# Loading and turning the first two context blocks during the folding stage of a Perceiver block

## The chip, the cores and the metric

The kernel runs on one core of a Trainium2 chip. Its engines work side by side, each through its own queue, in order: TensorE (PE in the profile; PEld is its weight load), VectorE (DVE), ScalarE (ACT), GpSimd (POOL) and SyncE (SP), which here only issues DMAs. ScalarE can issue DMAs too, from the same queue that holds its arithmetic. The metric is device time in microseconds (us), the median of several runs. The kernel before takes 2568.69 us (three runs, 2567.62 to 2571.4).

## The reference

`x` is 32 batches of 64 tokens with 256 channels; each batch has a context of 1601 keys with 192 channels. Three residual steps follow each other; only the first is touched by the change.

```python
x = x + xattn(layernorm(x), ctx, w_q, w_kv, w_out, b_out)
x = x + attn(layernorm(x), ...)      # a time-mixing recurrence over 64 tokens
x = x + ffn(layernorm(x), w1, b1, w2, b2)

def xattn(query, context, ...):      # 16 heads of 64
    q = query @ w_q                  # 256 -> 1024
    k, v = split(context @ w_kv)     # 192 -> 2 x 1024
    attn = softmax(q k^T / 8)        # per batch and head: 64 x 1601
    return (attn v) @ w_out + b_out
```

## The kernel before

Everything is float32. The keys are never projected. The key weights are folded into the queries instead: for each head, q (64 wide) times the transposed key weights gives a query of 192 channels, which meets the raw context. So the kernel has a first stage that folds, a long stage of attention, and a feed-forward stage at the end.

**Folding (`queries`, about 13 to 139 us).** The batches go in four groups of eight (`tg` = 0 to 3, 512 tokens each). A group has two halves (`e` = 0, 1) of eight heads. A half does, on TensorE: four head pairs projected (`q_ps`, L288), each copied out by ScalarE (L295) into one of five slots of the large tile `room[1]`; eight foldings onto the first 128 channels (`ql_ps`, L309), copied out in turn by VectorE (L316) and ScalarE (L317) into `q_lo`; the scores of the odd last key (`odd_ps`, L246) into `od`; and the foldings onto the other 64 channels (`qh_ps`, L337) into `q_hi`, mostly by VectorE (L344, L348). `q_ps` has two PSUM buffers, the others share six. `q_lo` (1 MB), `q_hi` (two halves of 0.5 MB) and `od` are stored to DRAM by SyncE (L319, L351, L260); `q_lo` and `q_hi` have two buffers each, so a copy waits for the store of the tile before the last. In the second half of groups 0, 1 and 2 the normalised x of the next group is turned (`xnT`, L208, L211), and VectorE normalises the group after that (L119 to L197).

**Context.** For every batch b the context comes three times: `ctx_load` (L143, tile `c`, 1152 KB, one buffer), used by the second product; `rows_load` (L152, four small DMAs) for the last 64 keys; and `blocks_load` (L170, tile `cb`, 12 DMAs of 96 or 104 KB in pieces of 128 bytes), which `ctx_prep` turns by four VectorE transposes (L368, L369) and one small DMA (L370) into `cT`, the context with channels on partitions, used by the scores. `q_load` (L180) brings the folded queries of a batch back.

**Attention (from about 139 us).** Two steps `u` per batch, eight heads each. A step computes scores in six pieces of 12 TensorE instructions (L654), each copied by ScalarE (L661) from one of two PSUM buffers; `rest_scores` (L631) takes one of these buffers too, in even steps between pieces 0 and 1. VectorE keeps a running maximum (L663 to L673), GpSimd reduces it over partitions (L680), VectorE subtracts it (L688, L699), ScalarE takes exponentials (L689, L700), VectorE sums (`total`, L773 to L777), GpSimd reduces the sum (L779), VectorE inverts it (`inverse`, L791 to L795), and a ScalarE-issued DMA stores the inverse (`keep`, L801). The products with the context follow one step later: `av_lo` (L464 with `c`, L816 with `rows`) and `av_hi` (L871, L826). Scores use two `s_sb` buffers; they are the same memory as `room[0]` and `room[1]`, and step 1 takes `room[1]`.

**What sets the order.** A scheduler orders each engine's instructions by program priority and data dependence; `tc.issue_after(x)` holds what stands under it until x has been issued in that order. All DMAs, from whichever engine, take eight completion counters in turn, and the compiled program makes a DMA wait until the DMA before it on its counter, eight back, has landed.

Of the kernel before, what the change touches and what calls it, by code (L numbers as in the profile page):

```python
# [15 lines left out]
P = 128  # L16
# [4 lines left out]
def kernel(  # L21
# [104 lines left out]
    with ExitStack() as st_b:  # L126
        with ExitStack() as st_a:
# [25 lines left out]
                            rows[b % 2][r0 : r0 + KR, n, n * C2 : P], ctx_768[b, KC * P : NK - 1, cs]  # L153
                        )

            def blocks_load(b):

                c = cpool.tile([P, NS, NBL, BL], F32, tag="cb", name=f"cb_{b}")
                for k in range(2):
                    n = (NB1, NBL)[k]
                    keys = slice(k * NB1 * BL, (k * NB1 + n) * BL)
                    for e in range(2):
                        a = 2 * k + e
                        for s in range(NS):
                            c0 = s * C2 + e * BL
                            nc.sync.dma_start(  # L170
                                c[a * BL : (a + 1) * BL, s, 0:n, :],
                                ctx_768[b, keys, c0 : c0 + BL].rearrange("(m q) r -> q m r", q=BL),
                            )
                return c
# [89 lines left out]
            def queries(tg, xnT, copied, sp, sps, wq_sb, wkT, room, codn, kodT, wk_lo, wk_hi, od):  # L264
# [7 lines left out]
                for e in range(NP // 4):  # L272
                    if e == 0 and more:
                        with tc.issue_after(copied.ins):
                            xn = normed_x(tg + 1, sp)
                    hi = sp.tile([P, QB, 4, T], F32, tag="q_hi", name=f"q_hi_{tg}_{e}", bufs=2)
                    qTs = []
                    for g in (2 * e, 2 * e + 1):
                        slot = (tg * NP // 2 + g) % 5
                        qT = room[1][:, slot * 2 * TG : (slot + 1) * 2 * TG].rearrange(  # L280
                            "p (k t) -> p k t", k=2
                        )
                        qTs.append(qT)
                        for k in range(2):
                            hp = 2 * g + k
                            pq = sps.tile([P, TG], F32, tag="ps", name=f"q_ps_{tg}_{hp}")
                            for c in range(2):
                                projected = nc.tensor.matmul(  # L288
                                    pq,
                                    lhsT=wq_sb[:, c, hp * P : (hp + 1) * P],  # L290
                                    rhs=xnT[:, c, :],
                                    start=(c == 0),
                                    stop=(c == 1),
                                )
                            nc.scalar.activation(qT[:, k, :], pq, AF.Copy, scale=HD**-0.5)  # L295
                    if e == 0 and tg == 0:
                        with tc.issue_after(projected.ins):
                            last_keys(codn, sps)
                    if e == 1 and more:
                        following = turned_x(tg + 1, xn, sp, sps)  # L300
                    for g, qT in zip((2 * e, 2 * e + 1), qTs):
                        lo = sp.tile([P, QB, 4, T], F32, tag="q_lo", name=f"q_lo_{tg}_{g}", bufs=2)
                        for k in range(2):
                            pl = [
                                sps.tile([P, QB, T], F32, tag="f", name=f"ql_ps_{tg}_{g}_{k}_{o}", bufs=6)
                                for o in range(2)
                            ]
                            for o in range(2):
                                nc.tensor.matmul(  # L309
                                    pl[o],  # L310
                                    lhsT=wkT[o * HD : (o + 1) * HD, 2 * g + k, 0:P],
                                    rhs=qT[o * HD : (o + 1) * HD, k, :],
                                    start=True,
                                    stop=True,
                                )
                            nc.vector.tensor_copy(lo[:, :, 2 * k, :], pl[0])  # L316
                            nc.scalar.copy(lo[:, :, 2 * k + 1, :], pl[1])  # L317
                        ns = slice(4 * g * T, (4 * g + 4) * T)
                        nc.sync.dma_start(  # L319
                            q_dram[tg][:, 0:P, ns].rearrange("b p n -> p b n"),  # L320
                            lo.rearrange("p b h t -> p b (h t)"),
                        )
                    all_q.append(qTs)
                    for n in (0, 1) if e == 1 and tg == 0 else (e,) if tg else ():
                        odd_scores(tg, n, kodT, all_q[n], od[n], sps)
                        if more:
                            odd_store(tg, n, od[n])
                        else:
                            odd_late.append(lambda n=n: odd_store(tg, n, od[n]))
                    for k in range(2):  # L330
                        ph = [
                            sps.tile([P, QB, T], F32, tag="f", name=f"qh_ps_{tg}_{e}_{k}_{o}", bufs=6)
                            for o in range(2)
                        ]
                        for n in range(2):
                            for o in range(2):
                                nc.tensor.matmul(  # L337
                                    ph[o][n * C2 : (n + 1) * C2, :, :],
                                    lhsT=wkT[o * HD : (o + 1) * HD, 4 * e + 2 * n + k, P:C],
                                    rhs=qTs[n][o * HD : (o + 1) * HD, k, :],  # L340
                                    start=True,
                                    stop=True,
                                )
                        nc.vector.tensor_copy(hi[:, :, 2 * k, :], ph[0])  # L344
                        if e == 1 and not more:
                            nc.scalar.copy(hi[:, :, 2 * k + 1, :], ph[1])
                        else:
                            nc.vector.tensor_copy(hi[:, :, 2 * k + 1, :], ph[1])  # L348
                    for n in range(2):
                        ns = slice((8 * e + 4 * n) * T, (8 * e + 4 * n + 4) * T)  # L350
                        store = nc.sync.dma_start(  # L351
                            q_dram[tg][:, P:C, ns].rearrange("b p n -> p b n"),
                            hi[n * C2 : (n + 1) * C2].rearrange("p b h t -> p b (h t)"),
                        )
                    if e == 0 and tg == 0:
                        for n in range(2):
                            projected_keys(n, wk_lo, wk_hi, kodT, sps)
                return following, store

            def ctx_prep(b):  # L360
# [12 lines left out]
            with tc.tile_pool(name="setup", bufs=1) as sp, tc.tile_pool(  # L373
# [11 lines left out]
                ]  # L385
                wk_hi, codn = wk_hi[0:C2], codn[0:B]
                kodT = kodT.rearrange("p (h b) -> p h b", b=B)
                od = kp.tile([P, NS * KT], F32, tag="cT", name="od")
                od = [
                    od[:, k * 2 * TG : (k + 1) * 2 * TG].rearrange("p (o t) -> p o t", o=2)  # L390
                    for k in range(2)
                ]
                wq_sb = wq_sb.rearrange("p (c n) -> p c n", c=2)
                wkT = wkT.rearrange("p (h c) -> p h c", c=C)
                wqr = w_q.rearrange("(c p) n -> p c n", p=P)
# [10 lines left out]
                for n in range(4, NT, 4):  # L406
                    nc.sync.dma_start(x_sb[:, n : n + 4, :], xr[:, n : n + 4, :])
                b_tiles = {0: blocks_load(0)}
                odd_late = []
                for g in range(NP // 2):  # L410
                    ps = sps.tile([P, 2, C], F32, tag="ps", name=f"wkT_ps_{g}")
                    for k in range(2):
# [8 lines left out]
                for tg in range(B // QB):  # L421
                    turned, store = queries(tg, *turned, sp, sps, wq_sb, wkT, room, codn, kodT, wk_lo, wk_hi, od)
                    if tg == 1:
                        q_tiles = {0: q_load(0)}
                        cT = ctx_prep(0)

            nats = {}
            aw = st_a.enter_context(tc.tile_pool(name="late", bufs=1))
# [539 lines left out]
                        x_sb[:, i, :], x_sb[:, i, :], bias_rows[:, 0, :], ALU.add  # L968
                    )

            c_tiles = {}
            rests = [None, None]
            last = None
            before = None
# [2 lines left out]
            for u in range(2 * B):  # L977
# [2 lines left out]
                phase, i = (u - 5) % 4, (u - 5) // 4  # L980
                if before is not None:
                    before.out()
                if j == 0:
                    rows_load(b)
                out, mixer, older = outs[max(i, 0)], mixers[max(i, 0)], mixers[max(i - 1, 0)]
                fill = {}
# [29 lines left out]
                s_sb, mx, top, done = scores(u, cT, q_tiles[b], hooks)  # L1016
                if j == 0 and b + 1 < B:
                    with tc.issue_after(store.ins):
                        b_tiles[b + 1] = blocks_load(b + 1)
                        q_tiles[b + 1] = q_load(b + 1)  # L1020
                mb = max_all(u, mx)
                if u == 1:
                    with tc.issue_after(top.ins):
                        cT_next = ctx_prep(1)
                if last is not None:
                    last.av_lo(fill, done)
                parts = exps(u, s_sb, rests[j], mb)
# [6 lines left out]
                    last.inverse()  # L1034
                    last.keep()
                if j == 0 and 0 < b < B - 1:
                    cT_next = ctx_prep(b + 1)
                elif j == 1:
                    cT = cT_next
                if phase == 0 and i > 0:  # L1040
# [4 lines left out]
                    out.vproj()  # L1045
                if phase == 1 and i >= 0:
                    mixer.norm()
                if j == 0:
                    c_tiles[b] = ctx_load(b)
                if phase == 3 and i >= -1:  # L1050
                    odd_load(i + 1)
# [150 lines left out]
```

## Time and profile before

| | |
|---|---|
| median of three runs | 2568.69 us |
| the profiled execution's own time | 2567.18 us |
| its span in the trace | 2565.4 us |
| TensorE busy | 2541.8 us, 99% |
| VectorE busy | 1925.2 us, 75% |
| ScalarE busy | 985.6 us, 38% |
| DMA on average | 68 GB/s; 190 GB/s over the first 230 us |

The page cuts the span in 40 slices; only the first three or four touch folding and the start of attention. Busy time is an average over stages. For a change at one place one asks what TensorE waits for at that place and which chain of work ends last there, in a window of the trace. "SPq" and "ACTq" are the queues of SyncE and ScalarE issuing DMAs. An arrow `<-` in a list of waits names what ended the wait.

### The profile page before, as it was taken

To read this page: it belongs to the slowest core of one execution; us is meant where nothing else is said; L and a number is where in the kernel's file an instruction comes from. 1 tells how busy PE (TensorE), PEld (TensorE's weight loads), DVE (VectorE), ACT (ScalarE), POOL (GpSimd) and SP (SyncE) were. 2 spreads that over 40 slices of the span, in tenths; PEclk is the share of its full clock that TensorE was granted. 3 is DMA by queue.
4 is the path that set the end of the run, shared out by engine and by line. 5 is a ranking of instruction groups with operands and counts; after the bars stand their busy time and mean duration, and the time that the engine had idled before them with its cause. 6 is when DMAs were issued, how large, how long until landed. Compare 5 with 4: busy or idle time off the path is not lost.

```text
span 2565.4 us, 38180 instructions
## 1 busy us (share of the span) xinstructions
PE 2541.8 (99%) x15650; PEld 1223.3 (48%) x15650; DVE 1925.2 (75%) x2364; ACT 985.6 (38%) x1104; POOL 410.7 (16%) x372
## 2 busy tenths in 40 slices
PE   9999999999999999999999999999999999999999
PEld 4334444444444444444444454444454444444466
DVE  5377777878787878878787878878787878787731
ACT  3343434334333434434433344343443334344221
POOL 1002111111111111111111111111111111111100
PEclk9999999999999999999999999999999999999999
DMA  7897332333232233233332323333332322310100
GB/s 189 225 210 112 62 62 51 66 65 65 53 69 56 49 58 65 47 66 66 65 63 57 61 40 65 54 59 66 65 65 53 69 55 48 62 45 4 53 13 21
DMA packets 435968, 174.24 MB, mean 68 GB/s; under 512 B 334960, under 2 KB 421520, under 8 KB 435792
## 3 DMA queue, kind: packets, MB, share of 16 engines
q1 hardware_dynamic: 435408, 171.53, 32.9%
q8 instruction: 123, 2.02, 0.3%
q14 instruction: 53, 0.43, 0.1%
q10 hardware_dynamic: 384, 0.26, 0.0%
HBM read 141.07 MB, written 29.10 MB: 66 GB/s over the span
## 4 chain that ended last, share of the span: by engine, by line
PE 90%; DVE 4%; issue 2%; SPq 1%; DMA 1%; POOL 1%; ACT 1%; ACTq 0%; DVEq 0%; POOLq 0%
PE s_ps L654 35%; PE o_lo L464 24%; PE o_hi L871 11%; PE y_ps L464 2%; PE q_ps L288 2%; PE h_ps L1113 2%; PE fy L1127 2%; PE rest_ps L631 2%; PE o_hi L826 1%; PE v_ps L924 1%; PE ql_ps L309 1%; DVE s_sb L699 1%; PE o_lo L816 1%; PE v_ps L938 1%; POOL den L779 1%
## 5 line engine op out<-in xcount | busy, mean ns | idle before, releaser
L654 PE MATMUL s_ps<-q,cT 64*128 64x512 f32 x4608 | 1008.1, 591 | 2.4 <-ACT s_sb L661 1.5
L654 PEld LDWEIGHTS s_ps<-q,cT 64*128 64x128 f32 x4608 | 443.7, 187 | 516.2 <-issue 497.5
L464 PE MATMUL o_lo<-s_sb,c 128*64 128x512 f32 x3024 | 680.3, 597 | 5.4 <-DMA c<-in_ctx_dram 5.4
L661 ACT COPY s_sb<-s_ps 128x1024 f32<-128x1024 f32 x384 | 388.3, 1011 | 744.8 <-PE s_ps L654 736.7
L699 DVE TENSOR_TENSOR s_sb<-s_sb,mb 128x2048 f32<-128x2048 f32 x192 | 431.5, 2284 | 0.0
L700 ACT ACTIVATE s_sb<-s_sb 128x2048 f32<-128x2048 f32 x192 | 367.2, 1913 | 123.6 <-DVE s_sb L699 123.6
L464 PEld LDWEIGHTS o_lo<-s_sb,c 128*64 128x64 f32 x3024 | 209.5, 137 | 387.0 <-issue 382.7
L665 DVE TENSOR_TENSOR m<-m,s_sb 128x1024 f32<-128x1024 f32 x256 | 312.3, 1220 | 45.4 <-ACT s_sb L661 24.2
L871 PE MATMUL o_hi<-s_sb,c 128*64 128x256 f32 x3024 | 337.7, 380 | 0.0
L776 DVE TENSOR_TENSOR t<-t,s_sb 128x1024 f32<-128x1024 f32 x256 | 311.9, 1218 | 8.6 <-DVE t L776 0.5
L871 PEld LDWEIGHTS o_hi<-s_sb,c 128*64 128x64 f32 x3024 | 217.9, 137 | 136.7 <-issue 37.1
L779 POOL PARTITION_ALL_REDUCE den<-t x64 | 207.1, 3236 | 400.2 <-issue 374.6
L791 DVE STREAM_TRANSPOSE turned<-den 128x512 f32<-128x512 f32 x64 | 45.5, 711 | 271.0 <-POOL den L779 271.0
L689 ACT ACTIVATE rest<-rest 128x512 f32<-128x512 f32 x64 | 40.4, 631 | 402.2 <-DVE rest L688 360.0
L680 POOL PARTITION_ALL_REDUCE mb<-m x64 | 114.2, 1785 | 427.4 <-DVE m L673 427.4
L688 DVE TENSOR_TENSOR rest<-rest,mb 128x512 f32<-128x512 f32 x64 | 44.3, 692 | 108.0 <-POOL mb L680 107.9
L619 POOL MEMSET rest<- 64x256 f32 x128 | 39.2, 307 | 418.3 <-PE o_lo L816 322.1
L368 DVE STREAM_TRANSPOSE cT<-cb 128x768 f32<-128x768 f32 x96 | 89.5, 957 | 0.0
L663 DVE TENSOR_TENSOR m<-s_sb 128x1024 f32<-128x1024 f32 x64 | 75.8, 1184 | 13.7 <-ACT s_sb L661 13.7
L816 PE MATMUL o_lo<-rest,rows 64*128 64x256 f32 x252 | 81.2, 402 | 0.0
L826 PE MATMUL o_hi<-rest,rows 64*128 64x256 f32 x252 | 81.2, 402 | 0.0
L111 POOL TENSOR_TENSOR rstd_ln<-rstd_ln,root 128x1 f32<-128x1 f32 (+1 forms) x24 | 33.1, 1380 | 296.9 <-DVE rstd_ln L110 279.1
(164 smaller groups left out, 1843.0 us busy)
## 6 DMA issues: line engine op xcount, KB each, us to landing
q<-q_dram SPq DMA_DIRECT2D x64, 768.0 KB
c<-in_ctx_dram SPq DMA_DIRECT2D x32, 1152.0 KB
cb<-in_ctx_dram SPq DMA_DIRECT2D x192, 104.0 KB
cb<-in_ctx_dram SPq DMA_DIRECT2D x192, 96.0 KB
q_dram<-q_lo SPq DMA_DIRECT2D x16, 1024.0 KB
q_dram<-q_hi SPq DMA_DIRECT2D x16, 512.0 KB
rows<-in_ctx_dram SPq DMA_DIRECT2D x64, 32.0 KB
rest<-o_dram SPq DMA_DIRECT2D x128, 1.0 KB
```

The costliest lines, as they stand in the source:

```text
L464: last = nc.tensor.matmul(out[rs], lhsT=lhsT[:, rs], rhs=rhs, start=start, stop=stop, skip_group_check=True,)
L654: done = nc.tensor.matmul(ps[:, k, :], lhsT=cT[rs, s, i * P : (i + 1) * P], rhs=q[rs, s, js : js + HALF], start=(s == 0), stop=(s == NS - 1),)
L661: copied = nc.scalar.copy(s_sb[:, 2 * i : 2 * i + 2, :], ps)
L665: nc.vector.tensor_tensor(m2, m2, s_sb[:, 2 * i : 2 * i + 2, :], ALU.max)
L680: nc.gpsimd.partition_all_reduce(mb, mx, P, bass_isa.ReduceOp.max)
L699: nc.vector.tensor_tensor(s, s, m, ALU.subtract)
L700: nc.scalar.activation(s, s, AF.Exp)
L776: nc.vector.tensor_tensor(t2, t2, p[:, 2 * i : 2 * i + 2, :], ALU.add)
L779: nc.gpsimd.partition_all_reduce(self.den, t2[:, 0, :], P, bass_isa.ReduceOp.add)
L816: nc.tensor.matmul(self.po[:, k * HH : (k + 1) * HH], lhsT=self.rows[lo, 0, :], rhs=self.rest[lo, k * HH : (k + 1) * HH], start=(k == 0), ...
L826: nc.tensor.matmul(self.ph, lhsT=self.rows.rearrange("p n c -> p (n c)")[hi, c0 : c0 + P], rhs=self.rest[hi, (1 - k) * HH : (2 - k) * HH], ...
L871: nc.tensor.matmul(self.ph[o * C2 : (o + 1) * C2, :], lhsT=self.ctx[:, self.at[c], P:C], rhs=self.s_sb[:, c, o * HH : (o + 1) * HH], start ...
```

## The change

`blocks_load` can take its room and its issuing queue from the caller. The blocks of batch 1 are loaded during group 0 of the folding, by 12 DMAs issued from ScalarE right after its copies into `q_lo` of the first half; they lie in a buffer of the tag `q`. `rows_load(0)` and `ctx_load(0)` are written at the end of group 2, where nothing that they need is late, and SyncE's compiled order has them, with the rows of batch 1, between the stores of group 0's two halves. `ctx_prep` runs for batch 0 after group 1 and for batch 1 after group 2, behind the last `q_hi` copies; in the kernel before, VectorE turned batch 0 within group 0 and batch 1 in step 1 of the attention, right after the maximum (`top`). The odd scores no longer lie in a `cT` buffer: the even half uses the memory of the running maximum `m2` (for group 3 a slot of `room[1]`), the other half the end of `room[1]`; in group 3 the even half is stored at once. The projections of a half (L288) may not be issued before the first folding of the half before (`folds`); in the kernel before the scheduler had moved them up between foldings, up to 11 matmuls at a time, where a half has eight. In the attention the loads that have gone are left out, and `ctx_prep(2)` waits for the maximum of step 2.

```diff
-            def blocks_load(b):
-                c = cpool.tile([P, NS, NBL, BL], F32, tag="cb", name=f"cb_{b}")
+            def blocks_load(b, room=None, queue=nc.sync):
+                if room is None:
+                    c = cpool.tile([P, NS, NBL, BL], F32, tag="cb", name=f"cb_{b}")
+                else:
+                    c = room.rearrange("p s n -> p (s n)")[:, 0 : NS * NBL * BL].rearrange(
+                        "p (s m r) -> p s m r", s=NS, r=BL
+                    )
...
-                            nc.sync.dma_start(
+                            queue.dma_start(
                                 c[a * BL : (a + 1) * BL, s, 0:n, :],
...
-                            for c in range(2):
-                                projected = nc.tensor.matmul(
+                            with tc.issue_after(folds[-1].ins) if folds else ExitStack():
+                                for c in range(2):
+                                    projected = nc.tensor.matmul(
...
-                                nc.tensor.matmul(
+                                fold = nc.tensor.matmul(
                                     pl[o],
...
-                            nc.scalar.copy(lo[:, :, 2 * k + 1, :], pl[1])
+                            laid = nc.scalar.copy(lo[:, :, 2 * k + 1, :], pl[1])
+                        if g == 2 * e:
+                            folds.append(fold)
...
                     for n in (0, 1) if e == 1 and tg == 0 else (e,) if tg else ():
+                        if not more and n == 0:
+                            at = (tg * NP // 2 - 1) % 5 * 2 * TG
+                            od[0] = room[1][:, at : at + 2 * TG].rearrange("p (o t) -> p o t", o=2)
                         odd_scores(tg, n, kodT, all_q[n], od[n], sps)
-                        if more:
+                        if more or n == 0:
                             odd_store(tg, n, od[n])
...
-                        nc.vector.tensor_copy(hi[:, :, 2 * k, :], ph[0])
+                        filed.append(nc.vector.tensor_copy(hi[:, :, 2 * k, :], ph[0]))
...
                             projected_keys(n, wk_lo, wk_hi, kodT, sps)
+                        cb = kp.tile([P, NS, H * T], F32, tag="q", name="cb_1")
+                        with tc.issue_after(laid.ins):
+                            b_tiles[1] = blocks_load(1, cb, nc.scalar)
...
-                od = kp.tile([P, NS * KT], F32, tag="cT", name="od")
-                od = [
-                    od[:, k * 2 * TG : (k + 1) * 2 * TG].rearrange("p (o t) -> p o t", o=2)
-                    for k in range(2)
-                ]
+                m2 = ap.tile([P, 2, HALF], F32, tag="m2", name="od")
+                od = [m2, room[1][:, 10 * TG : 12 * TG].rearrange("p (o t) -> p o t", o=2)]
...
                     if tg == 1:
                         q_tiles = {0: q_load(0)}
-                        cT = ctx_prep(0)
+                    if tg in (1, 2):
+                        with tc.issue_after(filed[-1].ins):
+                            cTs[tg - 1] = ctx_prep(tg - 1)
+                    if tg == 2:
+                        rows_load(0)
+                        c_tiles = {0: ctx_load(0)}
...
-            c_tiles = {}
+            cT, cT_next = cTs[0], cTs[1]
...
-                if j == 0:
+                if j == 0 and b:
                     rows_load(b)
...
                     with tc.issue_after(store.ins):
-                        b_tiles[b + 1] = blocks_load(b + 1)
+                        if b:
+                            b_tiles[b + 1] = blocks_load(b + 1)
                         q_tiles[b + 1] = q_load(b + 1)
                 mb = max_all(u, mx)
-                if u == 1:
-                    with tc.issue_after(top.ins):
-                        cT_next = ctx_prep(1)
...
                 if j == 0 and 0 < b < B - 1:
-                    cT_next = ctx_prep(b + 1)
+                    with tc.issue_after(top.ins) if b == 1 else ExitStack():
+                        cT_next = ctx_prep(b + 1)
...
-                if j == 0:
+                if j == 0 and b:
                     c_tiles[b] = ctx_load(b)
```

## The prediction

> **What bounds the kernel now.** I read the page first. TensorE is busy nearly all the time, so time can only come from its gaps and its slow stretches.
>
> ```profile
> span 2565.4 us, 38180 instructions
> PE 2541.8 (99%) x15650; PEld 1223.3 (48%) x15650; DVE 1925.2 (75%) x2364; ACT 985.6 (38%) x1104; POOL 410.7 (16%) x372
> ```
>
> Then the list of what TensorE waited for up to 204 us, where the change lies (us, times, longest), and the table by stretch (the last three numbers: granted clock, DMA share, GB/s).
>
> ```profile
> PE o_lo L464 <- DMA c<-in_ctx_dram: 5.4, 1, 5.4
> ...
> PE ql_ps L309 <- ACT q_lo L317: 1.2, 1, 1.2
> PE rest_ps L631 <- DMA cT<-cT: 1.1, 1, 1.1
> PE ql_ps L309 <- DVE q_lo L316: 1.0, 1, 1.0
> ...
> PE s_ps L654 <- ACT s_sb L661: 0.6, 1, 0.6
> 160.00:180.00 20.00, 14.56 (x68) 6.27 (x66) 17.71 (x15) 11.46 (x10) 2.01 (x2) 0.89 0.95 179
> ```
>
> The late `c` costs 5.4 us, and after that gap the clock is halved for a while: the 48 instructions of `o_lo` at 178.36 take 12.54 us, against 10.45 at 324 us. It looks as if 5.4 + 2.1 + 1.1 + 0.6 = 9.2 us were to be had. The chain that ends last says otherwise (start, us, what):
>
> ```profile
> 181.04 2.69 DVE cT L368 x3
> 183.76 0.37 DVE cT L369
> 184.17 0.69 DVE rest L688
> 184.86 6.60 DVE s_sb L699 x3
> ...
> 193.90 0.70 DVE t L777
> 194.76 3.23 POOL den L779
> ...
> 201.26 0.20 ACTq L801
> 201.50 1.02 ACT s_sb L661
> 202.57 13.14 PE s_ps L654 x60
> ```
>
> From 162 to 194.6 VectorE works without a pause; then come the sum over partitions, the inverse, and its store, which is a ScalarE instruction and stands before the first score copy of step 2. TensorE can't go past piece 0 and `rest_ps` without that copy. So VectorE's work, not `c`, decides when TensorE runs freely again, at 202.57.
>
> Last, the place where the new DMAs go: ScalarE's and TensorE's order around 30 us, and what SyncE waited for at 160 to 204 us.
>
> ```profile
> 25.28 0.58 ACT L317 COPY q_lo<-ql_ps 128x512 f32<-128x512 f32 x1 [0.27 <-PE ql_ps L309]
> 33.07 0.60 ACT L295 ACTIVATE room<-q_ps 128x512 f32<-128x512 f32 x1 [7.20 <-PE q_ps L288]
> ...
> 31.05 7.13 PE L288 MATMUL q_ps<-xnT,room 128*128 128x512 f32 x16
> ...
> SPq L444 <- DMA wv_lo<-in_L_xattn_w_kv_dram: 3.4, 1, 3.4
> SPq L260 <- DMA c<-in_ctx_dram: 3.2, 1, 3.2
> ```
>
> ScalarE is free for 7.2 us between two copies. The last two lines show DMAs held by others with which they share no data: each waits for the landing of the DMA eight before it.
>
> **The change, part by part** (+ is longer).
>
> *Start of step 2: -2.3.* The four transposes leave VectorE at 181.04 (3.1 us). Next late is the maximum over partitions: GpSimd has it at 181.31 + 1.78 = 183.1. In the new order a sum (L776, 1.24) fills part of that gap: sum to 182.3, L688 183.1 to 183.8, L699 to 190.4, sum to 191.7, L777 to 192.3, against 194.6. All behind it moves with it: TensorE at 200.3. Ends: -0.8 if the sum did not move up, -3.1 if the maximum came early.
>
> *The clock there: +2.1.* With `c` there, TensorE does the products from 172.9 at full rate (the exponentials that they read end at 170.7, 173.4 and 176.1, each ahead of its third): 10.45, then 5.2, to 188.5, then 0.6 + 2.6 + 1.5 of last rows, piece 0 and `rest_ps`, to 193.2. Then it idles 7.1 us, longer than the gap that cost 2.1, so I take 2.1; ends 0 and 3.4 (6.8 us of halved clock before, all of it used). The Trainium skill (TensorE: Matmul & The Clock Gate, Part 1) says that an idle window of about 3.4 us, running freely, halves the clock; the two halved windows after the 5.4 us gap agree. It speaks against the full gain, since the gap is moved, not removed: by it the sum below stands, and without it the sum would be 2.1 less.
>
> *Folding order: -2.3 and +1.7.* The two waits of 1.2 and 1.0 stand behind projections that were moved up, and go. But in the second halves of groups 0 and 1 VectorE now puts three `q_lo` copies (0.62 each) among the normalising, 1.9 us in 1.2 us of idle, so it ends at 46.05 for 45.34, and the fourth copy at 46.7. The buffer of that copy is wanted by `qh_ps`, which without projections in between is due at 45.8: 0.9 and 0.8. Ends 0 (copies hide) and 2.4.
>
> *The 12 DMAs on ScalarE: +4.7, and +1.0 of clock.* They stand between the copy that ends at 25.86 and the one due at 33.07. By the compiled order ScalarE's first waits for nothing late, but SyncE's eleventh block DMA of batch 0 now stands eight behind it, the first `q_lo` store comes after that on SyncE, and ScalarE's twelfth stands eight behind this store. So: first issued at 25.9, landed about 28.6 (the first weights, a larger load, took from 0.72 to 3.62); two block DMAs and the store issue until 30; the store landed 5.15 after issue (24.30 to 29.45 by the landing marks), so at 35.0 if nothing shares the DMA engines. What shares: block DMAs landed 0.76 apart, a 1 MB store took 3.9, so eleven plus two blocks and the store in a row end at 27.8 + 9.9 + 3.9 = 41.6. Middle 38.3. ScalarE then issues (0.3) and copies (0.6); TensorE, whose two `q_ps` buffers are full at 34.5, goes on at 39.2: 4.7, ends 1.4 and 8.0. A gap of this length costs half of the 2.1; ends 0 and 2.1. Behind ScalarE's DMAs wait the four `q_ps` copies and, through them, every folding of the half. The Trainium skill (DMA: Bandwidth & Descriptors, Issuing engines are not separate DMA queues) says that a second issuing engine saves issue time alone, since all DMAs share 16 engines. By that sentence alone the term would be 8.0 and the sum +8.9; no row of this run has two engines issuing much at once, so it can't be weighed closer here.
>
> *More in the DMA queues: +0.7.* `cb` (1.2 MB), `c` (1.15 MB) and eight row DMAs move into 26 to 50 us; SyncE issues nothing between 31 and 46.7, which covers the issues. What they push back are stores whose tiles are reused; VectorE waited 2.7 for such stores. I take a quarter; ends 0 and 2.7.
>
> *At nothing:* the eight transposes in groups 1 and 2 stand in the 6.9 us of four projections, where VectorE idled 5.0 or more after its copies; without that cover they would cost 3.1 each. ScalarE's first copy of step 1 (159.66) must now wait for four late odd stores in `room[1]`; they should land near 152, behind the last stores and `q_1`, and if they came after 159.7 each us would count. GpSimd's queue is as before, and the clearing that the row loads wait for (L107) is done at the start. The reloads for batches 2 and 3 come earlier, under steps in which TensorE never waited.
>
> Sum: -2.3 + 2.1 - 2.3 + 1.7 + 4.7 + 1.0 + 0.7 = +5.6. The profiled execution is 2567.2, 1.5 below the median; 2568.7 + 5.6 = 2574.3.
>
> **The rivals.**
>
> *The hold is short (not slower).* If the store lands at 35.0, TensorE goes on at 35.9: hold 1.4, no halved clock, no late stores: -2.3 + 2.1 - 2.3 + 1.7 + 1.4 = +0.6, 2569.3. For it: SyncE's issues cost 0.5 and the DMA engines are idle at 25 us. Against: nine more block DMAs are issued in that time. It decides where the store lands before 36.
>
> *The hold is long and stores fall behind.* 8.0 + 2.1 + 2.7 in place of 4.7 + 1.0 + 0.7: +12.0, 2580.7. For it: a DMA share of 0.8 to 0.98 in most of 60 to 160 us. Against: 0.50 at 40 to 60.
>
> *The whole 9.2 is won.* If VectorE's chain did not hold TensorE at step 2, then with a short hold: -9.2 - 2.3 + 1.7 + 1.4 = -8.4, 2560.3. Against: the chain above, link by link.
>
> **How the numbers follow.** A measurement can tell about 0.2%, 5.1 us, so slower begins at 2573.8 and faster at 2563.6. My forecast, own range 2570 to 2578, 0.50: its middle lies just above the bound, slower 0.29, within 0.21. Short hold 0.22: within 0.20, faster 0.02. Long hold 0.19: slower. Whole gain 0.09: faster 0.08, within 0.01. Together slower 0.48, within 0.42, faster 0.10. A range of 2566 to 2581 leaves out the whole gain, the far end of the short hold, and a little above.
>
> **What would show it.** ScalarE's first `q_ps` copy of group 0's second half starts at 36 to 41 (before 33.07), and TensorE's list has a wait of 1.4 to 8 for it there. No wait for `c` or for the turned context. TensorE waits some 7 us for `s_sb` L661 at the start of step 2, with a halved clock behind it. A free run through step 2, or ScalarE back by 34, would make the prediction wrong.

## Result and profile after

The changed kernel takes 2576.77 us in the median of seven runs (2573.37 to 2579.62), the kernel before 2568.69 on the same chip (seven runs, 2565.27 to 2573.22). The ratio is 1.0027, with a 95% interval of 1.0018 to 1.0037: slower by a little, and inside the predicted range. The profiled execution took 2574.45 us; its span of 2572.6 us is 7.2 us longer than that of before. TensorE is as full as it was: 2543.4 us busy, 99%.

What TensorE waited for in the changed kernel up to 300 us (total, times, longest):

```profile
PE s_ps L672 <- ACT s_sb L679: 7.9, 1, 7.9
PE q_ps L294 <- ACT room L301: 5.1, 1, 5.1
...
PE qh_ps L349 <- DVE q_lo L322: 1.9, 2, 1.1
```

The waits for `c`, for `cT` and for `q_lo` under `ql_ps` are gone. In their place stand 7.9 us at the start of step 2, 5.1 us behind the new DMAs, and 1.9 us before `qh_ps`. Both long ones begin at ScalarE. Its timeline in the changed kernel (start, duration, queue or engine, line, operation; in brackets the idle time before and what ended it):

```profile
25.38 15.57 ACTq L175 DMA_DIRECT2D cb<-in_ctx_dram  x12
41.00 1.09 ACT L301 ACTIVATE room<-q_ps 128x512 f32<-128x512 f32 x2 [15.04 <-DMA cb<-in_ctx_dram]
```

And TensorE's timeline there:

```profile
31.14 5.40 PE L294 MATMUL q_ps<-xnT,room 128*128 128x512 f32 x8
41.65 5.73 PE L294 MATMUL q_ps<-xnT,room 128*128 128x512 f32 x8 [5.12 <-ACT room L301]
```

Issuing the twelve DMAs keeps ScalarE for 15.6 us. The chain of the changed kernel in this window (start, us, what) says why:

```profile
26.98 1.94 ACTq L175
...
28.96 6.34 DMA cb<-in_ctx_dram
...
35.32 5.65 DMA cb<-in_ctx_dram
...
41.00 0.61 ACT room L301
```

ScalarE's last DMAs wait for the landing of other block DMAs, twice in a row, 6.3 and 5.7 us. The other place is the start of step 2, seen in ScalarE's timeline:

```profile
205.75 0.22 ACTq L819 DMA_DIRECT2D pd_dram<-rden  x1
206.01 1.01 ACT L679 COPY s_sb<-s_ps 128x1024 f32<-128x1024 f32 x1 [6.84 <-DVE rden L813]
```

and in TensorE's:

```profile
207.07 16.09 PE L672 MATMUL s_ps<-q,cT 64*128 64x512 f32 x60 [7.89 <-ACT s_sb L679]
```

TensorE has its data and stands 7.9 us at a copy that is queued behind the store `keep`; its clock is then halved, and the sixty score instructions take 16.09 us where they took 13.14 before. In the table by stretch (the last three numbers: granted clock, DMA share, GB/s) the clock is 0.74 there:

```profile
200.00:220.00 20.00, 12.93 (x48) 5.60 (x50) 13.66 (x18) 5.41 (x8) 6.31 (x4) 0.74 0.18 40
```

Where the 7.2 us come from, by the two traces (the line from first projection to first `xnT` is the second half of group 0):

| stretch | before | after | difference |
|---|---|---|---|
| start to that first projection | 31.05 | 31.14 | +0.1 |
| that projection to the first `xnT` of group 1 | 6.97 | 16.08 | +9.1 |
| from there to the first scores (rest of the folding) | 101.64 | 98.41 | -3.2 |
| first scores to step 2's sixty | 62.91 | 61.44 | -1.5 |
| step 2's sixty | 13.14 | 16.09 | +2.95 |
| sum | | | +7.4 |

### The profile page after: what moved, and what is told of

Its sections match the earlier page's. It is cut to its first block, busy times and chain, and to the rows that moved or that the text cites. A ratio compares the mean times of both kernels' runs of the same rounds, so it can differ in the third digit from the quotient of the medians.

```text
span 2572.6 us, 38172 instructions
## 1 busy us (share of the span) xinstructions
PE 2543.4 (99%) x15650; PEld 1223.5 (48%) x15650; DVE 1925.9 (75%) x2364; ACT 986.1 (38%) x1104; POOL 411.5 (16%) x372
## 4 chain that ended last, share of the span: by engine, by line
PE 90%; DVE 4%; issue 2%; DMA 2%; POOL 1%; SPq 1%; ACT 1%; ACTq 0%; DVEq 0%; POOLq 0%
PE s_ps L672 35%; PE o_lo L482 24%; PE o_hi L889 11%; PE y_ps L482 2%; PE q_ps L294 2%; PE h_ps L1130 2%; PE fy L1144 2%; PE rest_ps L649 2%; PE o_hi L844 1%; PE v_ps L942 1%; DVE s_sb L717 1%; PE ql_ps L315 1%; PE o_lo L834 1%; PE v_ps L956 1%; POOL den L797 1%
```

## Experiments

My theory: the twelve DMAs cost their hold of ScalarE and nothing else, and step 2 starts when ScalarE gets past `keep`, whatever has been loaded. The rivals: the extra transfers themselves cost; the new order on TensorE costs; the wait for `c` was on the path. Differences to the changed kernel are between medians; each comparison with the kernel before is against runs of it on the same chip. The kernel before had medians of 2568.69 to 2572.48 us in these sets of runs, so a difference between medians from two sets is sure to a few us only.

### The order alone, and the hold on top of it

The order alone, in the kernel before:

```diff
-                            for c in range(2):
-                                projected = nc.tensor.matmul(
+                            with tc.issue_after(folds[-1].ins) if folds else ExitStack():
+                                for c in range(2):
+                                    projected = nc.tensor.matmul(
...
-                                nc.tensor.matmul(
+                                fold = nc.tensor.matmul(
...
+                        folds.append(fold)
```

> The kernel before with the order on TensorE alone changed to the changed kernel's: projections never between the two foldings of a pair; no load is moved. My theory: the folding stretch from the first group's xnT to the first scores shrinks from 101.6 by about 3 us (1 to 4), and all of it reaches the end: 3 us under the kernel before. Rival, that the shorter stretch in the changed kernel came from the hold ahead of it (queues filled while TensorE stood): no change within 1 us.

Measured: 2570.24 us (11 runs), ratio 1.0004 (0.9993 to 1.0015). No change, but not for the rival's reason. TensorE's order is now that of the changed kernel; VectorE's is not. The scheduler keeps it as it was, with the copies into `q_lo` behind the whole normalising of the next group. TensorE's timeline in this run:

```profile
46.76 1.64 PE L310 MATMUL ql_ps<-room,room 64*128 64x512 f32 x2 [2.92 <-DVE q_lo L317]
48.34 3.05 PE L246 MATMUL odd_ps<-room,room 64*32 64x512 f32 x32
```

The stretch from the first `xnT` to the scores is 102.34 us. In it are 3.9 us of waits for `q_lo` and about 1.6 of slow clock (1.64 for 1.12, 3.05 for 1.95). What the regular order gains, VectorE's order takes.

The hold on top, in that kernel (its other loads held at their places with `issue_after(store.ins)`):

```diff
+                        cb = kp.tile([P, NS, H * T], F32, tag="q", name="cb_1")
+                        with tc.issue_after(laid.ins):
+                            blocks_load(1, cb, nc.scalar)
```

> The kernel before with the regular order of foldings (every projection follows the last folding) and the twelve block DMAs issued from ScalarE at the changed kernel's place, into a query buffer that nothing reads; the kernel's own loads all stay where they were. My theory: ScalarE held for about 15 us, TensorE idle about 5 us with its clock halved on both sides, about 9 us over the same kernel without the twelve DMAs (the run with the order alone), so about 6 us over the kernel before. Rival, that the hold is covered and the changed kernel loses elsewhere: within 2 us of the run with the order alone.

Measured: 2577.85 us (8 runs), ratio 1.0028 (1.0017 to 1.0038); 7.6 us over the order alone. ScalarE's queue is held 16.89 us, TensorE stands 4.88, and the first `xnT` comes at 48.69 where it came at 38.70. Of these 10.0 us, 1.2 lie ahead of the projections (32.89 for 31.73) and are not the hold's; 3.8 come back in the folding (98.51 for 102.34): with the DMAs in ScalarE's queue, the scheduler puts VectorE's copies among the normalising, as in the changed kernel, and TensorE no longer waits for them. The hold is the loss, and a better order of VectorE comes with it.

### The blocks on SyncE's queue

```diff
-                            b_tiles[1] = blocks_load(1, cb, nc.scalar)
+                            b_tiles[1] = blocks_load(1, cb, nc.sync)
...
-                        if g == 2 * e:
-                            folds.append(fold)
+                        folds.append(fold)
```

> The changed kernel with one thing different: the twelve DMAs of the second batch's blocks are issued from SyncE's queue instead of ScalarE's (the order on TensorE is pinned to that of the changed kernel by making every projection follow the last folding). My theory, ScalarE held by its own issues: the gap of 5.1 us before the second eight projections and the halved clock around it go, the stretch from the first projections to the next xnT falls from 16.1 to about 7 us, the time is about 9 us under the changed kernel's (about 1 under the kernel before's). Rival 1, the extra transfers themselves cost: the stretch stays above 14 us and the time stays within 2 us of the changed kernel's. Rival 2, SyncE's queue is now too full and its query stores come late: the stretch falls, but waits of up to 9 us for the copies into q_lo appear in the folding.

Measured: 2579.32 us (5 runs), ratio 1.0034 (1.0021 to 1.0047): no gain at all. The hold is gone (first `xnT` at 39.18, no wait before the projections), as the theory said, though the sixteen projections take 8.83 us and not the 7 expected; but the folding behind it takes 107.7 us for 98.4. The waits:

```profile
PE ql_ps L315 <- DVE q_lo L322: 5.8, 2, 2.9
PE s_ps L671 <- ACT s_sb L678: 5.7, 1, 5.7
...
PE o_lo L481 <- ACT s_sb L717: 3.2, 1, 3.2
```

The first is VectorE's order of the run above, twice, each with a halved clock behind it. So SyncE's queue was not yet cleared of blame; the next run tells the two apart.

```diff
-                    if e == 0 and more:
-                        with tc.issue_after(copied.ins):
-                            xn = normed_x(tg + 1, sp)
...
-                            nc.vector.tensor_copy(lo[:, :, 2 * k, :], pl[0])
+                            laid_lo = nc.vector.tensor_copy(lo[:, :, 2 * k, :], pl[0])
...
+                    if e == 0 and more:
+                        with tc.issue_after(laid_lo.ins):
+                            xn = normed_x(tg + 1, sp)
                     all_q.append(qTs)
```

> The run with the blocks on SyncE's queue again, with VectorE's order mended: the normalisation of the next group's rows is issued behind the copies into q_lo of the first half instead of ahead of them. If the waits of 2.9 us for q_lo and the halved clock behind them were VectorE's order and nothing of the loads, they go, the folding stretch is at most 98.5 us (107.7 in that run), scores start at 136 to 139, and the time is 7 to 10 us under the changed kernel's. If they come from the loads in SyncE's queue, the stretch stays above 104.

Measured: 2569.97 us (11 runs), ratio 1.0000 (0.9991 to 1.0009); 6.8 us under the changed kernel, just short of the 7 to 10. No wait for `q_lo` is left, and the folding stretch is 96.17 us. It was VectorE's order. The scores start at 138.88, and then 4.4 us are lost again: 65.8 us to step 2's sixty for 61.4. The chain of this run shows where:

```profile
173.24 3.42 DMA b_sb<-in_L_ffn_b_dram
...
176.67 0.02 ACTq L709
...
177.48 1.02 ACT s_sb L678
```

`L709` (L710 in the changed kernel) is ScalarE's store of step 0's remainder exponentials. It shares no data with `b_sb`, a small late load that SyncE issues; yet it is issued only when that load has landed, and step 1's score copies stand behind it for 6.4 us.

### The store in front of step 2

```diff
-                def keep(self):
+                def keep(self, queue=nc.scalar):
...
                 if u == 1:
                     last.total()
                     last.inverse()
-                    last.keep()
+                    last.keep(nc.sync)
```

> The changed kernel with one thing different: in step 1 the store of the first half's inverted sums (keep) is issued from SyncE's queue instead of standing in ScalarE's ahead of step 2's score copies. My theory, that this store is what step 2 waits for: the gap of 7.9 us at the start of step 2 and the halved clock behind it go, 8 to 11 us under the changed kernel's time. Rival, that the copies would wait anyway, for the exponentials or for VectorE: the gap keeps more than 5 us and the time falls by under 4 us.

Measured: 2566.38 us (11 runs), ratio 0.9988 (0.9979 to 0.9997); 10.4 us under the changed kernel, from one DMA of 2 KB on another queue. By the two traces about 9.5 of this lie between the first scores and the end of the sixty (54.83 and 13.15 us for 61.44 and 16.09). The sixty start at 198.99 and run at full clock:

```profile
198.99 13.15 PE L672 MATMUL s_ps<-q,cT 64*128 64x512 f32 x60 [0.46 <-ACT s_sb L679]
```

The same edit in the kernel before:

> The kernel before, with the store of the first half's inverted sums in step 1 moved from ScalarE's queue to SyncE's, and nothing of the change. My theory: with c late the store is barely ahead of TensorE (0.65 us of wait for the score copy), so 0 to 1.5 us under the kernel before: early loads and the moved store pay only together. Rival, that the store costs the same in both kernels: 8 us or more under.

Measured: 2569.8 us (11 runs), ratio 1.0000 (0.9991 to 1.0008): nothing. The wait for `c` (5.5 us) is still there and covers the store. And the other half alone, the early `c` in the kernel before:

```diff
                     if tg == 1:
                         q_tiles = {0: q_load(0)}
                         cT = ctx_prep(0)
+                        rows_load(0)
+                        c_tiles = {0: ctx_load(0)}
```

(with `if j == 0 and b` for the loads in the loop, as in the change). The loads are written at the end of group 1 (`tg` = 1) here; the change writes them at the end of group 2, the place that the expectation names.

> The kernel before with one part of the change alone: the first batch's context c and its rows are loaded in the folding (after group 2's work) and not at the end of step 0. My theory, that step 2 starts when ScalarE gets past the store of the inverted sums and not when c has come: the wait of 5.4 us for c goes, TensorE reaches the same place 7 us earlier and stands there as much longer, its clock is halved behind that gap, and the time is 0 to 4 us over the kernel before's. Rival, that the wait for c is on the path: 5 to 8 us under the kernel before.

Measured: 2576.95 us (5 runs), ratio 1.0033 (1.0020 to 1.0045), 6.4 us over the kernel before: on the side of the theory, but over its 0 to 4. The wait for `c` is gone, and from the first scores to the sixty it still takes 62.93 us (62.91 before):

```profile
201.81 1.53 PE L633 MATMUL rest_ps<-q,cT 64*64 64x256 f32 x24 [3.46 <-DMA cT<-cT]
...
209.19 15.25 PE L656 MATMUL s_ps<-q,cT 64*128 64x512 f32 x60 [5.85 <-ACT s_sb L663]
```

So `c` alone is worth 0.0 there, and the slow clock costs 2.1. The part that I had not expected lies earlier: the folding takes 107.95 us for 101.64. The load is issued at 94.8, and the stores of `q_lo` behind it land late (ScalarE's list of waits in this run, up to 210 us):

```profile
ACT q_lo L317 <- DMA q_dram<-q_lo: 11.1, 3, 7.5
```

In the kernel before this line has 1.6. In the changed kernel it does not appear; there SyncE issues `c` at 45.3, while ScalarE and TensorE have just come out of the hold. So the loss in the folding goes with where this run loads, and what it shows of the change is the stretch from the first scores on.

### GpSimd beside VectorE

```diff
                     for i in range(2, KC // 2):
-                        nc.vector.tensor_tensor(t2, t2, p[:, 2 * i : 2 * i + 2, :], ALU.add)
+                        with tc.issue_after(taken[-1].ins) if u == 0 and i == 4 else ExitStack():
+                            nc.vector.tensor_tensor(t2, t2, p[:, 2 * i : 2 * i + 2, :], ALU.add)
...
-                    nc.vector.tensor_tensor(rest, rest, mb, ALU.subtract)
+                    taken.append(nc.vector.tensor_tensor(rest, rest, mb, ALU.subtract))
```

> The changed kernel with one sum of VectorE (L794, the third of four) issued behind GpSimd's maximum in step 1 instead of beside it. If a sum of two tiles on VectorE keeps GpSimd from running, the maximum takes 1.8 us again (2.6 in the changed kernel, 1.8 in the kernel before) and VectorE's rest starts 0.8 us sooner after it; the sums' end is then 0.4 us later and the time within 2 us of the changed kernel's. If the maximum takes 2.6 here too, its length has another cause (the transfers of that time).

Measured: 2575.33 us (10 runs), ratio 1.0018 (1.0009 to 1.0027) to the kernel before; 1.4 under the changed kernel's median, which is no difference between two sets of runs. GpSimd's timeline, the changed kernel first, then this run:

```profile
187.28 2.60 POOL L698 PARTITION_ALL_REDUCE mb<-m  x1 [8.09 <-DMA cb<-in_ctx_dram]
```

```profile
189.37 1.78 POOL L698 PARTITION_ALL_REDUCE mb<-m  x1 [8.08 <-DVE m L691]
```

The maximum takes 1.78 us when the sum does not run beside it. From the last maximum on VectorE to `rest` it is 2.0 us here, 2.8 in the changed kernel. The other traces agree: the maximum of this step takes 2.60 us in all seven in which that sum runs beside it, and 1.78 in this run and in the six in which VectorE turns tiles there. TensorE gains nothing by it: from the first scores to the sixty it is 61.87 us here and 61.44 in the changed kernel, since the sum now stands behind.

### All together, and without the loads

Blocks from SyncE, VectorE's order, and `keep` from SyncE:

> The changed kernel with all three: blocks from SyncE's queue, VectorE's normalisation behind the copies, and the store of the first half's inverted sums from SyncE's queue. If the costs add as they were measured one by one: about 10 us under the run without the moved store, 17 to 19 under the changed kernel, 8 to 11 under the kernel before. If they cover one another: no more than 11 under the changed kernel.

Measured: 2562.33 us (11 runs), ratio 0.9973 (0.9964 to 0.9982); 14.4 under the changed kernel, between the two expectations. Against the run without the moved `keep` it is 7.6 us, not 10: the 3.8 us behind `L709` are still there. So that store goes too:

```diff
-                        nc.scalar.dma_start(
+                        (nc.scalar if u else nc.sync).dma_start(
                             pd_dram[b, 0, h0 : h0 + NP // 2].rearrange("h t -> (h t)").unsqueeze(0),
```

> The run with all three, and in step 0 the two stores of the first half's remainder to pd_dram go from SyncE's queue too. There ScalarE's queue stood at these stores for 6.7 us (its chain shows them behind the landing of a small load from SyncE's queue) and TensorE waited 3.8 us for the exponentials behind them. If that is the whole cause: the 3.8 us go, the stretch from the first scores to step 2's sixty falls from 58.8 to 54 or 56 us, and the time is 3 to 5 us under the run with all three. If the copies behind the stores wait for something else (the landing of the odd store into the same room): within 1.5 us of it.

Measured: 2555.36 us (5 runs), ratio 0.9938 (0.9925 to 0.9952). The stretch from the first scores to the sixty falls from 58.8 to 55.0 us, as expected; the medians, from two chips, differ by more, 7.0 us; the two profiled executions differ by 4.3, and the traces do not show the rest. What TensorE waits for up to 230 us in this run, after the first projections:

```profile
PE s_ps L671 <- ACT s_sb L678: 1.3, 1, 1.3
PE s_ps L671 <- ACT q_hi L357: 0.8, 1, 0.8
```

Last, the same kernel beside one in which all loads are where the kernel before has them:

> The run before last (everything moved off ScalarE's queue, VectorE's order mended) without the change's early loads: the kernel before with the regular order on TensorE, VectorE's normalisation behind the copies, and the two kinds of stores on SyncE's queue. If the early loads of the change are worth what stood in the list of waits (5.4 for the late c, about 2 of clock behind it, 1.1 for the turned context), this run is 6 to 10 us over the run with them and about 5 under the kernel before. If the waits only move here too, it is within 2 us of the run with them.

> The run with the early loads and nothing on ScalarE's queue once more, on the same chip as the run without the loads, so that the two can be set side by side: 2553 to 2557 us, no wait over 1.5 us from the first scores to the end of step 2.

Measured on one chip: 2562.23 us without the early loads (8 runs, ratio 0.9969, 0.9959 to 0.9980) and 2553.28 with them (5 runs, ratio 0.9935, 0.9922 to 0.9947). The early loads are worth 9.0 us here, 6.9 of it by the two traces between the first scores and the end of the sixty. The kernel without them is itself 7.8 us under the kernel before, where 5 had been expected: so much do the mended orders and the moved stores give alone. In this kernel TensorE's list of waits has both old lines again:

```profile
PE rest_ps L633 <- DMA cT<-cT: 4.9, 1, 4.9
...
PE o_lo L466 <- DMA c<-in_ctx_dram: 0.9, 1, 0.9
```

So the loads of the change are a gain once ScalarE's queue holds no DMA ahead of a copy that TensorE needs. Part of it shows already with the hold still there: moving `keep` alone gave nothing in the kernel before (ratio 1.0000) and took the changed kernel to 0.9988 (0.9979 to 0.9997). The last version is the fastest of all: 16.7 us under the kernel before.

## Why the prediction was right, and where it was not

The sign, the size (+5.6 forecast, +7.4 by the traces, +8.1 by the medians) and the two places came out as predicted. That the sum came so near is in part luck: the clock around the hold was 3.0 more than predicted and the folding order 2.6 less, and these two errors nearly cancel. Term by term:

| term | predicted | measured |
|---|---|---|
| start of step 2 | -2.3 | -1.5 |
| the clock there | +2.1 | +2.95 |
| folding order, both parts | -0.6 | -3.2 |
| hold of ScalarE | +4.7 | +5.1 |
| clock around the hold | +1.0 | +4.0 |
| later stores | +0.7 | 0.0 |

*Start of step 2.* The mechanism is shown: early `c` alone gains 0.0, `keep` on another queue gains 10.4 in the changed kernel and nothing in the kernel before. The -1.5 is the transposes' leaving step 1. What was mis-sized is "the maximum over partitions: 1.78": it took 2.60 beside the sum that I had let run there. The run with that sum later shows the missing 0.8 (and, with 61.87 us to the sixty, 1.0 under before where the prediction's end for a sum that did not move up was 0.8). The Trainium skill (SBUF — State Buffer, SBUF: two separate sides) says that a VectorE operation with two SBUF inputs and a GpSimd operation that reads SBUF can't hold their shared port pair together, and that the later one waits for the whole of the other. The rows agree: the sum runs from 187.03 to 188.25, the maximum is due at 187.28, and 2.60 - 1.78 = 0.82 is most of that overlap of 0.97. I had not weighed this rule.

*The clock there.* TensorE idled 7.9 us for the predicted 7.1, and lost 2.95 of the possible 3.4.

*Folding order.* The two parts that I had named came as said: the old waits of 1.2 and 1.0 are gone, and `qh_ps` waits 1.05 and 0.88 for the predicted 0.9 and 0.8. What failed is a step that was left out: without its waits the stretch is 96.5 us (98.41 - 1.93), and in the kernel before 99.4 (101.64 - 2.26). The run with VectorE's order mended, without any such wait, has 96.17. TensorE's own work got 2.9 us shorter when projections no longer stood between foldings. An unbroken row of sixteen `ql_ps` instructions takes 3.70 us, but one folding split from its partner (x2) takes 1.05 by itself. The same fourteen instructions, in the kernel before and then in the changed kernel:

```profile
70.70 2.84 PE L309 MATMUL ql_ps<-room,room 64*128 64x512 f32 x10
...
74.53 1.12 PE L309 MATMUL ql_ps<-room,room 64*128 64x512 f32 x2
76.69 1.12 PE L309 MATMUL ql_ps<-room,room 64*128 64x512 f32 x2 [1.04 <-DVE q_lo L316]
```

```profile
80.63 3.70 PE L315 MATMUL ql_ps<-room,room 64*128 64x512 f32 x14
```

By the starts of what follows, the broken row costs 1.2 more, and the four other broken rows of foldings 0.2 to 0.3 each, about 2.1 together; the broken rows of projections cost some 0.7 more in all. These rows were in the trace of before, and I had not priced them.

*Hold.* 5.1 for 4.7, inside the ends, but the working was right only in part. The rule that a DMA waits for the one eight back is what held ScalarE; the transfer was not the first `q_lo` store but earlier block DMAs, two rounds of about 6 us. ScalarE was back at 41.0 and not at 38.6, and TensorE had filled its buffers only at 36.5 and not at 34.5, because its clock was halved; the two errors nearly cancel, which is luck. One window of the changed kernel (the last three numbers again clock, DMA share, GB/s) has both causes:

```profile
32.13:35.54 3.41, 3.41 (x6) 1.33 (x5) 0.00 (x0) 0.00 (x0) 0.00 (x0) 0.50 1.15 349
```

The DMA share is 1.13 to 1.15 in this and the next two windows, up to 42.37, so the engines were busy throughout, and ScalarE's return at 41.0 is nearer to 41.9, which the working gives if all transfers share the engines, than to its middle of 38.6. The Trainium skill's sentence (DMA: Bandwidth & Descriptors, Issuing engines are not separate DMA queues), that DMAs from all issuers run on the same 16 engines, agrees with that. By it alone the term was put at 8.0; with TensorE's buffers full at 34.5 it would have been about 7 (41.65 - 34.5), and it was 5.1.

*Clock around the hold.* The term that was mis-sized most: 5.40 and 5.73 us for the two rows of eight projections, which take 3.56 each at full clock: +4.0. The second, +2.2, follows the gap and belongs to it, but not every such gap costs it: in the run with only `keep` moved in the changed kernel the gap was 3.8 us, and the eight behind it took 3.70. The first, +1.8, does not belong to the gap: it begins at 32.1, ahead of it. The same sixteen projections took 7.13 in the kernel before, 8.83 in the first run with the blocks on SyncE and 9.31 in the run of the kernel before with only `keep` moved, which is the kernel before up to there; neither has a hold. All 14 traces fit one reading. The granted clock changes on a grid of 3.41 us that lies differently in each execution, and just ahead of the projections stands the row of narrow `kod_ps` matmuls. In the nine traces with slow projections one interval of the grid held 2.49 us or more of that row (2.49 in the changed kernel), and the clock was halved from its end on; in the five others no interval held more than 2.47 (2.26 in the kernel before). So this part came, as far as the traces tell, with the execution and not with the change; no run moved the row to try it.

*Later stores.* No copy in the changed kernel waits for a store of `q_lo`. The place of `c` in SyncE's queue is the likely reason: in the run with early `c` alone, issued at 94.8, such waits came to 11.1 us on ScalarE; the place by itself was not tried. That rival, the stores that fall behind, was real, but not here.

*The rivals.* The short hold was refuted by ScalarE's return at 41.0 (the bound was 36). The whole 9.2 was not won. Once ScalarE's queue was free the early loads gained 9.0, but that this is so near 9.2 is chance in part: the waits that went there were 4.9 for `cT` and 0.9 for `c`, not 1.1 and 5.4.

## What to carry to other kernels

A DMA issued from an engine that computes is an instruction in its queue: ask not what the transfer costs but what it waits for (its data, and the DMA before it on its completion counter) and what arithmetic stands behind it. A wait taken off the list gains only as much as the next chain allows; look for the instruction that ends that chain, and move it as well, or the gap only moves. When a scheduler sets the order, compare the order on every engine and not only on the one that was edited: here VectorE's order was worth as much as the loads.

## What was not expected of the hardware

- A maximum over partitions on GpSimd took 2.60 us beside a VectorE sum of two SBUF tiles (seven traces) and 1.78 without it (seven traces, in six of them beside VectorE transposes, which read one tile).
- The same sixteen projections at 30 to 34 us took 7.13, 8.83 or 9.31 us in different profiled executions of kernels with no wait there; in the slower ones the granted clock is 0.5 to 0.6 from 32.13 to 35.54. They follow the narrow `kod_ps` matmuls (32 columns). Where that row falls on the grid on which the clock changes separates the slow from the fast in all 14 traces; it was not tried by moving the row.
- Twelve DMAs of about 100 KB held ScalarE's queue for 15.6 us, behind the landing of other block DMAs, and two stores of 1 KB held it for up to 6.7 us, behind a load of another queue with which they share no data.
